# Table-lookup convolution block on one core: norm and gate matmuls in other places, a 128x128 gate, second-layer centring on GpSimd

## The chip, the cores and the metric

One NeuronCore of a Trainium2 chip runs the kernel. The metric is device time in microseconds (us) of one execution. The engines are called TensorE (PE for its matmuls, PEld for its weight loads), VectorE (DVE), ScalarE (ACT), GpSimd (POOL) and SyncE (SP, which here issues most DMAs). SBUF is the on-chip memory of 128 partitions, PSUM the eight banks that TensorE writes.

## The reference

For 16 images of 256 channels and 28x28 pixels the block is

```
x0  = group_norm(x, 32 groups)
out = relu(bn1(amm_conv3x3(x0, centroids1, wsub1)))
out = bn2(amm_conv3x3(out, centroids2, wsub2))
s   = sigmoid(relu(mean(out) @ se_w1 + se_b1) @ se_w2 + se_b2)     # 256 -> 16 -> 256
y   = x + relu(out * s + x0)
amm_conv3x3: p = 3x3 patches per channel (9 values), 16 centroids per channel
  attn = softmax(-|p - centroid|^2)            # over the 16 centroids
  lut  = centroids . wsub                      # per channel: 16 x 256
  out  = sum over channels and centroids of attn * lut
```

All is float32. The kernel does not build the lookup table: the softmax-weighted mean of a channel's centroids is a vector of nine values, and these, multiplied with `wsub`, give the same sum.

## The kernel before, in words

One image is cut into four blocks, `hh` (which 128 channels) by `t` (upper or lower half, 14 rows, N = 392 pixels). The order is `BLOCKS = ((0,0),(0,1),(1,1),(1,0))`. For a block:

- `patches` copies shifted rows of the image from DRAM (`home1`, `home2`) into one of two SBUF buffers `pts[0]`, `pts[1]`; `logits` (line 349) multiplies them with block-diagonal centroids `wd` in 32x32 tiles of TensorE into eight PSUM banks `lg`; `exps` (line 361, ACT) makes `e`.
- `num_b` (`nb`, line 410) gives the softmax sums and the ninth value, `num_a` (`na`, line 396) the other eight values in four pairs. DVE takes a reciprocal and spreads it (`rb`, lines 447 and 451). POOL multiplies (`scale_q`, line 459: `qo` and two of the `qp` pairs) and DVE the other two pairs (line 470).
- `product` (line 478, `acc`) is the convolution proper: nine 128x128 weights times the nine values. The four blocks are combined with seven products in place of eight (S1 to S4, A11, A12, A22); `mix` (lines 485 and 487, POOL) forms the differences of blocks that these need, `combine` (line 188, DVE) the sums of weights. `acc_copy`, `acc_add` (line 515) and `reg_add` put the products together (`half_sum`, `hpad`, `y`).

A PSUM bank comes from one ring of eight, which logits, numerators, products and all small matmuls share: a new one waits until the reader of the bank eight before it is done.

Every step is put on a list with `at(cluster, sub, function, ...)` and issued in order of (cluster, sub). Each engine runs its own instructions in that order. A block starts every two clusters and an image every eight, so `g = 8 * n` is the first cluster of image `n` (0 to 15 is layer 1, 16 to 31 layer 2), and sub orders the steps in a cluster: patches 0.5, logits 0.1 to 0.3, `nb` and `na` 1.0 to 1.45, spread and scale 1.7 to 1.8, product 2.0, mixes 1.75 and 2.5. So a cluster is, for TensorE: logits, then (in the even ones) `nb`, then `na`, then one product.

Beside this run, once per image or once in all:

- Group norm of the next image: `gn_stats` (line 284), `gn_mean` (a matmul of one column pair, line 290, then DVE `gn_gm`, `gn_dv` in lines 294 to 297), `gn_var` (matmul, line 303, then DVE and four small POOL operations, `rsqrt`), `gn_apply` on ACT, `to_home1`. For image 0 they stand ahead of the list, channel half by channel half.
- Squeeze and excitation in layer 2: `se_hidden` (four matmuls, line 750, and ACT) and `se_gate` (two matmuls, line 763, ACT, and DVE in lines 771 and 772).
- Centring of `wd`, so that logits need no norm of the patch: `center_sq` (square, line 251), `center_add` (matmul `sqp` with `nhalf_sb`, line 256, and addition), `center_mean` (line 261 to 263). Both halves of layer 1's weights are centred on DVE ahead of the list. Layer 2's are sorted by a ranking of the channels and centred during images 5 and 6 (`prep_wd2`, `prep_wd3`, `prep_wd4`, clusters 43 to 51).
- Loads of weights, the gate's among them, at the start on SP's and POOL's queues.

Of the kernel before, what the change touches and what calls it, by code (L numbers as in the profile page):

```python
# [8 lines left out]
F32 = mybir.dt.float32  # L9
I32 = mybir.dt.int32  # L10
U32 = mybir.dt.uint32
AF = mybir.ActivationFunctionType
# [5 lines left out]
P = 128  # L18
# [7 lines left out]
K = 16  # L26
# [41 lines left out]
def kernel(  # L68
# [80 lines left out]
    def load(ap, name, eng=None):  # L149
        t = const.tile(list(ap.shape), ap.dtype, name=name)  # L150
        (eng or nc.sync).dma_start(t, ap)
        return t
# [42 lines left out]
    load_wd(None, 1)  # L195
    load_cw(0, 1)
    vecs = load(vec, "vecs", nc.gpsimd)
    w1_sb = const.tile([P, NB, RED], F32, name="w1_sb")
    nc.gpsimd.dma_start(w1_sb, se_w1.rearrange("(b p) r -> p b r", p=P))
    w2_sb = load(se_w2, "w2_sb", nc.gpsimd)  # L200
    b1_sb = const.tile([RED, 1], F32, name="b1_sb")
    nc.gpsimd.dma_start(b1_sb, se_b1.rearrange("(p o) -> p o", o=1))

    m_lo, m_hi, zero = kst[:, 0:1], kst[:, 1:2], kst[:, 2:3]
    m_cw = kst[:, 3:7]
# [40 lines left out]

    cst = const.tile([P, 64], F32, name="cst")

    def center_sq(wf, c0, w):
        sq = rpool.tile([P, N], F32, tag="r", name="sq")  # L250
        nc.vector.tensor_mul(sq[:, :w], wf[:, c0 : c0 + w], wf[:, c0 : c0 + w])
        return sq

    def center_add(wf, c0, w, sq):
# [1 line left out]
        nc.tensor.matmul(ps[:, :w], lhsT=nhalf_sb, rhs=sq[:, :w], start=True, stop=True)  # L256
        nc.vector.tensor_add(wf[:, c0 : c0 + w], wf[:, c0 : c0 + w], ps[:, :w])

    def center_mean(wf, n):
        g = wf.rearrange("p (g k) -> p g k", k=K)  # L260
        nc.vector.tensor_reduce(cst[:, : n // K], g, axis=AX.X, op=ALU.add)
        nc.vector.tensor_scalar_mul(cst[:, : n // K], cst[:, : n // K], 1.0 / K)
        nc.vector.tensor_sub(g, g, cst[:, : n // K].unsqueeze(2).to_broadcast([P, n // K, K]))

    def center(wf, n):
        for c0 in range(0, n, 256):
# [57 lines left out]
    def to_home1(b, k, half=None):  # L324
        if k == NB - 1:
            xs.pop(b)
        p0, p1 = (0, P) if half is None else (64 * half, 64 * half + 64)
        nc.sync.dma_start(home1[b][k * P + p0 : k * P + p1], twice(xpads[k][p0:p1]))
# [41 lines left out]
    def wide_turn(u, mm):  # L370
        z = io.tile([P, 4 * N], F32, tag="pb", name="z")
        nc.vector.transpose(z, u["e", mm].rearrange("p i n -> p (i n)"))
        mx = small.tile([P, N // 4], F32, name="mx")
        zk = z.rearrange("p (g k) -> p g k", k=K)
        nc.vector.tensor_reduce(mx, zk, axis=AX.X, op=ALU.max)
        u["z", mm] = z, mx
# [296 lines left out]
            )  # L673

    def prep_wd2(part):
        pw["sq"] = center_sq(pw["st"][:, 512:1536], 384 * part, min(384, 1024 - 384 * part))

    def prep_wd3(part):
        center_add(pw["st"][:, 512:1536], 384 * part, min(384, 1024 - 384 * part), pw["sq"])

    def prep_wd4():
        st = pw.pop("st")
        center_mean(st[:, 512:1536], 1024)
        f = st[:, 512:1536].rearrange("p (g n) -> p g n", n=32)
        nc.vector.tensor_sub(f, f, kbias.unsqueeze(1).to_broadcast([P, 32, 32]))
        nc.sync.dma_start(d_wd[1], st[:, 512:1536])

    def prep_cw0():
# [55 lines left out]
    def se_hidden(b):  # L744
        ysum = ys[b, "sum"]
        ps = bank("sep")[:, :1]
        n = 0
        for k in range(NB):
            for i in range(2):
                nc.tensor.matmul(  # L750
                    ps[0:RED], lhsT=w1_sb[:, k, :], rhs=ysum[:, k, i : i + 1],
                    start=(n == 0), stop=(n == 2 * NB - 1),
                )
                n += 1
        hid = small.tile([RED, 1], F32, name="se_hid")
        nc.scalar.activation(hid, ps[0:RED], AF.Relu, bias=b1_sb, scale=1.0 / HW)
        se[b] = hid

    def se_gate(b):
# [74 lines left out]
    def at(cl, sub, f, *a, **kw):  # L834
        jobs.setdefault((cl, sub), []).append((f, a, kw))
# [54 lines left out]
    for l in range(2):  # L890
        for b in range(B):
            n = l * B + b
            g = 8 * n
            us = blocks[4 * n : 4 * n + 4]
            for c, (w, r, ks) in PRODUCTS.items():
                at(g + c, 2.0, product, (n, c), us[r], w, ks)
            for mm in (4, 2, 3, 0, 1):
                at(g + 5, 2.5, mix, us[0], mm, us[1], us[0])
                at(g + 7, 2.5 if mm < 2 else 1.75, mix, us[1], mm, us[2], us[1])
                at(*((g + 7, 2.6) if n < B - 1 else (g + 8, 1.0)), mix, us[0], mm, us[2], us[0])  # L900
                at(g + 10, 1.0, mix, us[0], mm, us[0], us[3])
            c11, c12, c21, c22 = (0, 0), (0, 1), (1, 0), (1, 1)
            at(g + 6, 0.0, acc_copy, l, b, c11, (n, 5))
            at(g + 7, 0.0, acc_copy, l, b, None, (n, 6))
            at(g + 8, 0.0, acc_add, l, b, None, (n, 7))
            at(g + 9, 0.0, acc_add, l, b, c21, (n, 8), c11)
            at(g + 10, 0.0, acc_add, l, b, c22, (n, 9), c11, pop=False)
            at(g + 10, 0.01, acc_add, l, b, c21, (n, 9))
            at(g + 10, 0.05, reg_add, l, b, c12, c22, None)
            at(g + 10, 0.06, reg_add, l, b, c22, c21, None)  # L910
            at(g + 11, 0.0, acc_add, l, b, c12, (n, 10))
            at(g + 11, 1.9, norm_out, l, b, *c12)
            at(g + 11, 1.91, norm_out, l, b, *c22)
            at(g + 12, 0.0, acc_add, l, b, c11, (n, 11))
            at(g + 12, 0.3, norm_out, l, b, *c11)
            at(g + 13, 0.0, acc_add, l, b, c21, (n, 12), op=ALU.subtract)
            at(g + 13, 0.3, norm_out, l, b, *c21)
            if l == 0:
                for o in range(2):
                    if b == 0:  # L920
                        at(g + 12 + o, 0.35, rank_score, o)
                        at(g + 12 + o, 0.6, rank_keep, o)
                        at(g + 12 + 2 * o, 0.65, h0_keep, o)
                    else:
                        for r in range(2):
                            at(g + 12 + o + (o and r), (0.5, 2.9)[r] if o == 0 else (2.4, 2.9)[r], to_home2, b, o, r)
                if b + 1 < B:
                    at(g + (-1 if b else 2), 2.6, load_x, b + 1)
                    for q in range(NB):
                        at(g + (1 + 2 * q if b else 4), 0.3, gn_stats, b + 1, q)  # L930
                    at(g + 4, 1.05 if b else 1.96, gn_mean, b + 1)
                    at(g + 4, 1.33 if b else 1.97, gn_var, b + 1)
                    for q in range(NB):
                        at(g + 5, 0.9, gn_apply, b + 1, q)
                        at(g + 5, 1.9, to_home1, b + 1, q)
            else:
                last = b == B - 1
                at(*((g + 11, 0.6) if last else (g + 13, 2.6)), load_x, b, last)
                at(g + 13, 2.1, se_hidden, b)
                at(g + (14 if last else 15), 1.05, se_gate, b)  # L940
                for q in range(NB):
                    at(g + (13 if last else 19), 0.9, finish_norm, b, q)
                    if not last:
                        at(g + 19, 0.91, finish_gate, b, q)
                        at(g + 20, 0.05, finish_sum, b, q)
                        at(g + 20, 0.9, finish_relu, b, q)
                        at(g + 21, 0.05, finish_add, b, q)
                        at(g + 21, 0.06, store, b, q)
                    else:
                        at(g + 14, 1.92, finish_fast, b, q)  # L950
                        at(g + 14, 1.92, store, b, q)
                if b == B - 1:
                    at(g + 11, 0.95, flags)
                    at(g + 12, 2.9, flag_sum)

    at(1, 0.6, load_w, 0, "A11")
    at(3, 0.6, load_w, 0, "S3")
    at(3, 0.6, load_w, 0, "A22")
    at(6, 0.6, load_w, 0, "A12")
    for c, m in ((5, "S1"), (7, "S2"), (8, "S4"), (6, "S3")):  # L960
        at(c, 1.96, combine, m)
# [21 lines left out]
    for part in range(3):  # L983
        at(43 + 2 * part, 1.9, prep_wd2, part)
        at(44 + 2 * part, 1.05, prep_wd3, part)
    at(51, 0.3, prep_wd4)
    at(52, 0.6, prep_cw0)
    at(53, 1.9, prep_cwa)
    for part in range(4):
        at((59, 60, 67, 68)[part], 2.3, prep_cwb, part)  # L990
    for n in range(5):
        at(70 + 2 * n, 0.6, sums_load, 2 * n)
        at(71 + 2 * n, 2.3, sums_put, 2 * n)
# [10 lines left out]
    at(g + 4, 0.6, load_w, 1, "A12")  # L1004
    at(g + 5, 0.6, load_w, 1, "A22")

    for k in range(NB):
        gn_stats(0, k)
        gn_mean(0, k, 1)
        gn_var(0, k, 1)  # L1010
        gn_apply(0, k)
        if k == 0:
            for i in range(2):
                to_home1(0, 0, i)
            nc.vector.memset(pts[0], 1.0)
            nc.gpsimd.memset(pts[1], 1.0)
    for hh in range(2):
        center(wts["wd", hh].rearrange("p a b c -> p (a b c)"), 512)
    at(-0.5, 0.7, to_home1, 0, 1)
    at(0, 1.95, setup_bn)  # L1020
    for t in hpads:
        at(1, 1.95, nc.gpsimd.memset, t, 0.0)

# [157 lines left out]
```

## Time and profile before

| | us |
|---|---|
| runs | 2762.52, 2751.57, 2767.31 (median 2762.52) |
| the profiled execution | 2760.28 |
| its span, first to last instruction | 2758.7 |
| busy in it: PE | 2674.9 (97%) |
| POOL | 2066.8 (75%) |
| DVE | 1732.6 (63%) |
| ACT | 1454.4 (53%) |

The profile is of one execution. A row of its timeline gives the start in us, the duration in us, engine, line, operation, output and inputs, shapes and how many instructions are merged (xN); in square brackets stands how long the engine was idle before it and what ended that. A matmul in float32 appears as two passes. Durations in groups of one kind are given as a mean in ns. PE's share of busy time says little of its speed, since matmuls overlap; what counts is when the next group can start.

### The profile page before, as it was taken

To read this page: it belongs to the slowest core of one execution; us is meant where nothing else is said; L and a number is where in the kernel's file an instruction comes from. 1 tells how busy PE (TensorE), PEld (TensorE's weight loads), DVE (VectorE), ACT (ScalarE), POOL (GpSimd) and SP (SyncE) were. 2 spreads that over 40 slices of the span, in tenths; PEclk is the share of its full clock that TensorE was granted. 3 is DMA by queue.
4 is the path that set the end of the run, shared out by engine and by line. 5 is a ranking of instruction groups with operands and counts; after the bars stand their busy time and mean duration, and the time that the engine had idled before them with its cause. 6 is when DMAs were issued, how large, how long until landed. Compare 5 with 4: busy or idle time off the path is not lost. (4 is left out here: it accounts for less than half of the span.)

```text
span 2758.7 us, 87946 instructions
## 1 busy us (share of the span) xinstructions
PE 2674.9 (97%) x37076; PEld 1297.7 (47%) x37076; DVE 1732.6 (63%) x3950; ACT 1454.4 (53%) x3277; POOL 2066.8 (75%) x1420
## 2 busy tenths in 40 slices
PE   5989999799999999999999999999999999999997
PEld 2444444344444444444444444444444444444443
DVE  5765555765555565565576766676766666766664
ACT  4444455445455445455455466656566656556653
POOL 4756787738877767766678777888877788877787
PEclk9999999999999999999999999999999999999998
DMA  9665677546677656666585455445555545555541
GB/s 202 149 135 136 165 191 184 146 107 158 154 189 189 157 128 151 158 160 150 117 183 122 105 123 122 111 104 114 114 123 123 115 104 113 116 117 123 117 105 47
DMA packets 223025, 374.51 MB, mean 136 GB/s; under 512 B 30152, under 2 KB 193336, under 8 KB 222624
## 3 DMA queue, kind: packets, MB, share of 16 engines
q1 hardware_dynamic: 215392, 334.50, 53.8%
q0 software_dynamic: 7232, 34.30, 3.6%
q8 instruction: 296, 4.85, 0.8%
q14 instruction: 105, 0.86, 0.1%
HBM read 288.91 MB, written 79.80 MB: 134 GB/s over the span
## 5 line engine op out<-in xcount | busy, mean ns | idle before, releaser
L361 ACT ACTIVATE e<-lg 128x392 f32<-128x392 f32 x1920 | 777.7, 530 | 822.7 <-PE lg L349 821.7
L487 POOL TENSOR_TENSOR qp<-qp,qp 128x784 f32<-128x784 f32 x512 | 938.2, 1862 | 41.8 <-DVE qp L470 41.8
L478 PE MATMUL acc<-qp,w_S 128*128 128x392 f32 x2048 | 709.0, 497 | 5.3 <-POOL qp L487 5.2
L459 POOL TENSOR_TENSOR qp<-qp,rb 128x784 f32<-128x784 f32 x256 | 473.0, 1869 | 253.6 <-DVE rb L451 253.6
L349 PE MATMUL lg<-pt,wd 32*32 32x392 f32 x16384 | 533.5, 503 | 28.8 <-DVE half_sum L515 17.3
L451 DVE STREAM_SHUFFLE rb<-r 128x392 f32<-128x392 f32 x1024 | 550.8, 605 | 0.0
L478 PEld LDWEIGHTS acc<-qp,w_S 128*128 128x128 f32 x2048 | 388.5, 191 | 296.7 <-POOL qp L487 10.9
L478 PE MATMUL acc<-qp,w_A 128*128 128x392 f32 x1536 | 521.3, 493 | 0.0
L396 PE MATMUL na<-e,cwa 64*32 64x392 f32 x8192 | 412.1, 498 | 10.0 <-issue 9.8
L430 DVE SCALAR_TENSOR_TENSOR r<-nb,kst,r 128x392 f32<-128x392 f32 x128 | 79.8, 624 | 517.5 <-ACT r L421 510.6
L478 PEld LDWEIGHTS acc<-qp,w_A 128*128 128x128 f32 x1536 | 292.5, 190 | 213.1
L410 PE MATMUL nb<-e,cwb 64*32 64x392 f32 x8192 | 372.2, 497 | 0.0
L349 PEld LDWEIGHTS lg<-pt,wd 32*32 32x32 f32 x16384 | 230.9, 103 | 282.8 <-issue 179.6
L436 DVE RECIPROCAL r<-r 128x392 f32<-128x392 f32 x128 | 331.9, 2593 | 0.0
L459 POOL TENSOR_TENSOR qo<-qo,rb 128x392 f32<-128x392 f32 x128 | 131.1, 1024 | 220.3 <-DVE rb L447 220.2
L470 DVE TENSOR_TENSOR qp<-na,rb 128x392 f32<-128x392 f32 x512 | 252.4, 555 | 56.1 <-PE na L396 53.1
L396 PEld LDWEIGHTS na<-e,cwa 64*32 64x32 f32 x8192 | 145.2, 106 | 234.6 <-ACT e L361 123.5
L410 PEld LDWEIGHTS nb<-e,cwb 64*32 64x32 f32 x8192 | 146.2, 107 | 209.2 <-issue 126.5
L464 ACT COPY qp<-na 128x392 f32<-128x392 f32 x512 | 211.8, 512 | 10.9 <-PE na L396 10.8
L421 ACT ACTIVATE r<-nb,kst 128x392 f32<-128x392 f32 x128 | 87.5, 684 | 102.3 <-PE nb L410 99.8
L367 ACT COPY e<-lg 128x392 f32<-128x392 f32 x128 | 52.9, 500 | 152.9 <-PE lg L349 152.9
L485 POOL TENSOR_TENSOR qo<-qo,qo 128x392 f32<-128x392 f32 x128 | 130.8, 1022 | 2.2
(143 smaller groups left out, 1778.1 us busy)
## 6 DMA issues: line engine op xcount, KB each, us to landing
pt<-home SPq DMA_DIRECT2D x768, 209.0 KB
pt<-home SPq DMA_DIRECT2D x753, 104.5 KB
home<-xpad SPq DMA_DIRECT2D x31, 899.0 KB
xt<-in_x SPq DMA_DIRECT2D x30, 784.0 KB
out_dram<-y SPq DMA_DIRECT2D x32, 392.0 KB
w_S<-d_wS SPq DMA_DIRECT2D x4, 576.0 KB
st<-in_wsub SPq DMA_DIRECT2D x4, 512.0 KB
st<-d_wa SPq DMA_DIRECT2D x16, 128.0 KB
```

What stands on the lines that cost most here:

```text
L349: nc.tensor.matmul(bk[32 * c : 32 * c + 32, :N].rearrange("p (r w) -> p r w", w=W), lhsT=wts["wd", u["hh"]][32 * i : 32 * i + 32, mm, c, : ...
L361: nc.scalar.activation(eg[:, i, :], bk[:, :N], AF.Exp, scale=2.0)
L396: nc.tensor.matmul(bs[r][32 * i : 32 * i + 32, :N], lhsT=wts["cwa", u["hh"]][64 * r : 64 * r + 64, mm, i, :], rhs=es[64 * r : 64 * r + 64, ...
L410: nc.tensor.matmul(bs[r][32 * i : 32 * i + 32, :N], lhsT=wts["cwb", u["hh"]][64 * r : 64 * r + 64, mm, i, :], rhs=es[64 * r : 64 * r + 64, ...
L436: nc.vector.reciprocal(u["r"], u["r"])
L451: nc.vector.stream_shuffle(rb[:, r, :], u["r"], mask_of(2 * mm + r))
L459: nc.gpsimd.tensor_tensor(q, q, u.pop(("rb", mm)), ALU.mult)
L464: nc.scalar.copy(u["q", 2 * mm + r], bk[:, :N])
L470: nc.vector.tensor_mul(u["q", 2 * mm + r], bk[:, :N], rb[:, r, :])
L478: nc.tensor.matmul(accs[key][:, :N], lhsT=wl[w][:, k, :], rhs=us["q", k], start=first and n == 0, stop=last and n == len(ks) - 1,)
L485: nc.gpsimd.tensor_tensor(out_u["q", 8], in0["q", 8], in1["q", 8], ALU.subtract)
L487: nc.gpsimd.tensor_tensor(pair(out_u, mm), pair(in0, mm), pair(in1, mm), ALU.subtract)
```

## The change

- The normalisation of image 0 goes half by half with the centring: norm of half 0, centring of `wd` half 0, norm of half 1; the centring of half 1 goes into cluster 0 of the list. `pts[0]` is filled with ones in two parts.
- The gate's weights are loaded in cluster 92, by SP, into 128x128 and 128x256 tiles that POOL clears before; the first of them reuses `nhalf_sb`. `se_hidden` and `se_gate` multiply with 128 rows and columns.
- `gn_mean` and `gn_var` of the next image go from `g+4` (1.05 and 1.33) to after the products of `g+3` and `g+4`; `se_gate` from `g+15`, 1.05 to after the product of `g+14`.
- In image 0 the first product goes from cluster 5 to 4, and its copy with it.
- In layer 2's centring the squares and two of the subtractions go from DVE to POOL.
- `load_w` and `load_x` of the start get other subs in their clusters; `mx` has one buffer for two.

```diff
-    w1_sb = const.tile([P, NB, RED], F32, name="w1_sb")
-    nc.gpsimd.dma_start(w1_sb, se_w1.rearrange("(b p) r -> p b r", p=P))
-    w2_sb = load(se_w2, "w2_sb", nc.gpsimd)
-    b1_sb = const.tile([RED, 1], F32, name="b1_sb")
-    nc.gpsimd.dma_start(b1_sb, se_b1.rearrange("(p o) -> p o", o=1))
+    w1_sb = [nhalf_sb, const.tile([P, P], F32, name="w1_sb")]
+    w2_sb = const.tile([P, C], F32, name="w2_sb")
+    b1_sb = const.tile([P, 1], F32, name="b1_sb")
+
+    def load_se():
+        for t in (*w1_sb, w2_sb, b1_sb):
+            nc.gpsimd.memset(t, 0.0)
+        for k in range(NB):
+            nc.sync.dma_start(w1_sb[k][:, :RED], se_w1[k * P : (k + 1) * P, :])
+        nc.sync.dma_start(w2_sb[:RED], se_w2)
+        nc.sync.dma_start(b1_sb[:RED], se_b1.rearrange("(p o) -> p o", o=1))
...
-    def center_sq(wf, c0, w):
+    def center_sq(wf, c0, w, eng=None):
-        nc.vector.tensor_mul(sq[:, :w], wf[:, c0 : c0 + w], wf[:, c0 : c0 + w])
+        (eng or nc.vector).tensor_mul(sq[:, :w], wf[:, c0 : c0 + w], wf[:, c0 : c0 + w])
...
-    def center_mean(wf, n):
+    def center_mean(wf, n, eng=None):
-        nc.vector.tensor_sub(g, g, cst[:, : n // K].unsqueeze(2).to_broadcast([P, n // K, K]))
+        (eng or nc.vector).tensor_sub(g, g, cst[:, : n // K].unsqueeze(2).to_broadcast([P, n // K, K]))
...
-        mx = small.tile([P, N // 4], F32, name="mx")
+        mx = small.tile([P, N // 4], F32, name="mx", bufs=1)
...
     def prep_wd2(part):
-        pw["sq"] = center_sq(pw["st"][:, 512:1536], 384 * part, min(384, 1024 - 384 * part))
+        pw["sq"] = center_sq(pw["st"][:, 512:1536], 384 * part, min(384, 1024 - 384 * part), nc.gpsimd)
...
-        center_mean(st[:, 512:1536], 1024)
+        center_mean(st[:, 512:1536], 1024, nc.gpsimd)
         f = st[:, 512:1536].rearrange("p (g n) -> p g n", n=32)
-        nc.vector.tensor_sub(f, f, kbias.unsqueeze(1).to_broadcast([P, 32, 32]))
+        nc.gpsimd.tensor_sub(f, f, kbias.unsqueeze(1).to_broadcast([P, 32, 32]))
...
-                    ps[0:RED], lhsT=w1_sb[:, k, :], rhs=ysum[:, k, i : i + 1],
+                    ps, lhsT=w1_sb[k], rhs=ysum[:, k, i : i + 1],
...
-        hid = small.tile([RED, 1], F32, name="se_hid")
-        nc.scalar.activation(hid, ps[0:RED], AF.Relu, bias=b1_sb, scale=1.0 / HW)
+        hid = small.tile([P, 1], F32, name="se_hid")
+        nc.scalar.activation(hid, ps, AF.Relu, bias=b1_sb, scale=1.0 / HW)
...
-                at(g + c, 2.0, product, (n, c), us[r], w, ks)
+                at(g + c - (c == 5 and n == 0), 2.0, product, (n, c), us[r], w, ks)
...
-            at(g + 6, 0.0, acc_copy, l, b, c11, (n, 5))
+            at(g + (6 if n else 5), 0.0, acc_copy, l, b, c11, (n, 5))
...
-                    at(g + (-1 if b else 2), 2.6, load_x, b + 1)
+                    at(*((g - 1, 2.6) if b else (2, 1.65)), load_x, b + 1)
                     for q in range(NB):
-                        at(g + (1 + 2 * q if b else 4), 0.3, gn_stats, b + 1, q)
-                    at(g + 4, 1.05 if b else 1.96, gn_mean, b + 1)
-                    at(g + 4, 1.33 if b else 1.97, gn_var, b + 1)
+                        at(g + (1 + q if b else 4), 0.3, gn_stats, b + 1, q)
+                    at(g + (3 if b else 4), 2.1, gn_mean, b + 1)
+                    at(g + 4, 2.1 if b else 2.2, gn_var, b + 1)
                     for q in range(NB):
-                        at(g + 5, 0.9, gn_apply, b + 1, q)
-                        at(g + 5, 1.9, to_home1, b + 1, q)
+                        at(g + 5, 0.9 if b else 0.3, gn_apply, b + 1, q)
+                        at(g + 5, 1.9 if b or q else 0.9, to_home1, b + 1, q)
...
-                at(g + (14 if last else 15), 1.05, se_gate, b)
+                at(g + 14, 1.05 if last else 2.1, se_gate, b)
...
-    at(1, 0.6, load_w, 0, "A11")
-    at(3, 0.6, load_w, 0, "S3")
-    at(3, 0.6, load_w, 0, "A22")
+    at(1, 1.65, load_w, 0, "A11")
+    at(3, 1.65, load_w, 0, "S3")
+    at(3, 1.65, load_w, 0, "A22")
...
-    at(51, 0.3, prep_wd4)
+    at(51, 1.9, prep_wd4)
...
+    at(92, 2.3, load_se)
...
-    for k in range(NB):
+    def norm0(k):
         gn_stats(0, k)
         gn_mean(0, k, 1)
         gn_var(0, k, 1)
         gn_apply(0, k)
-        if k == 0:
-            for i in range(2):
-                to_home1(0, 0, i)
-            nc.vector.memset(pts[0], 1.0)
-            nc.gpsimd.memset(pts[1], 1.0)
-    for hh in range(2):
+
+    def center_wd(hh):
         center(wts["wd", hh].rearrange("p a b c -> p (a b c)"), 512)
+
+    nc.vector.memset(pts[0][:, :4], 1.0)
+    norm0(0)
+    for i in range(2):
+        to_home1(0, 0, i)
+    nc.vector.memset(pts[0][:, 4:], 1.0)
+    nc.gpsimd.memset(pts[1], 1.0)
+    center_wd(0)
+    norm0(1)
+    at(0, 1.95, center_wd, 1)
     at(-0.5, 0.7, to_home1, 0, 1)
-    at(0, 1.95, setup_bn)
+    at(0, 1.96, setup_bn)
```

## The prediction

> **What bounds the kernel now.** I read the page first, then the busy time by stretches, then the timeline where TensorE (PE) stood still.
>
> ```profile
> PE 2674.9 (97%) x37076; PEld 1297.7 (47%) x37076; DVE 1732.6 (63%) x3950; ACT 1454.4 (53%) x3277; POOL 2066.8 (75%) x1420
> ```
>
> ```profile
> 0.00:64.00 64.00, 32.72 (x580) 14.20 (x596) 33.15 (x89) 24.91 (x55) 28.22 (x47) 0.93 0.98 207
> 535.00:562.00 27.00, 11.63 (x165) 3.83 (x164) 18.79 (x9) 4.68 (x11) 16.97 (x10) 0.62 0.35 81
> 562.00:1500.00 938.00, 934.09 (x12990) 454.97 (x12990) 566.16 (x1372) 474.69 (x1081) 686.82 (x508) 1.00 0.64 154
> 1500.00:2740.00 1240.00, 1239.38 (x17184) 606.83 (x17183) 821.61 (x1778) 718.33 (x1606) 998.87 (x601) 1.00 0.50 111
> ```
>
> The second table's columns are the stretch, its length, busy PE, weight load, DVE, ACT, POOL, then PE clock, DMA share, GB/s. From 562 us on, PE is idle for 4.5 us in 2178: there only PE's own instructions count. What waiting there is to win lies ahead of 64 us, where the DMA engines are 98% busy, and between 535 and 562 us. The timeline of that second hole, with DVE, POOL and PE in order of start (us, then duration):
>
> ```profile
> 535.52 16.73 DVE L251 TENSOR_TENSOR sq<-st 128x256 f32<-128x256 f32 x1
> ...
> 536.62 3.63 POOL L459 TENSOR_TENSOR qp<-qp,rb 128x784 f32<-128x784 f32 x2
> ...
> 544.77 7.20 POOL L487 TENSOR_TENSOR qp<-qp,qp 128x784 f32<-128x784 f32 x4
> 552.18 0.55 DVE L515 TENSOR_TENSOR half_sum<-acc,half_sum 128x392 f32<-128x392 f32 x1
> 552.78 1.53 PE L349 MATMUL lg<-pt,wd 32*32 32x392 f32 x8 [15.37 <-DVE half_sum L515]
> ```
>
> One square of 256 columns holds DVE for 16.73 us, until POOL's unbroken row of products ends at 551.97; alone the same size took 0.41 us (L251 at 14.56 us). half_sum stands behind it, and PE waits for the bank that half_sum empties.
>
> **Part 1: centring on POOL.** From lg at 535.49 to the next acc at 561.79 PE takes 26.3 us; undisturbed rows (lg 1.96, sqp 0.9, nb 2.66, na 1.48) make 7.0. The hole costs 19.3 us, the slow clock behind it included, and it goes, since no DVE square is left there. POOL's squares then come late themselves: in POOL's order each stands behind two qp products (L459). The third follows those of 536.62, which end at 540.25; at 1.02 us per 128x392 (L485) it takes 0.7 and ends at 541.0. PE wants it at 537.4, with nb and na queued behind: 3.6 us. A 3.51 us gap at 293.66 us also ran the next eight matmuls in 4.59 us instead of 2.7, so 5.5. The first square is 0.6 us late in the same way, the second is not. Net -13.2 (from -19, if POOL's backlog is gone, to -8).
>
> The Trainium skill (SBUF — State Buffer, "SBUF: two separate sides") says that a DVE instruction with two SBUF inputs and a GpSimd one that reads SBUF exclude each other for a whole instruction. The hole at 535.52 agrees; but by that rule a wait lasts one instruction, some 2 us, and part 1 would then be worth little.
>
> The two subtractions of 1024 columns also go to POOL, in image 6. Before they took DVE 1.23 us each with PE never idle. On POOL, by 1862 ns for 784 columns, they take 2.4 each (by the broadcast z row, 2.87 for 1568, 1.9), starting near 600 us. Just then DVE must do gn_dv (L296, two SBUF inputs) and behind it hpad, whose bank the next lg wants 1.5 us into its group. So gn_dv can be held 1 to 5 us: +4.5 (0 to 6.5). The d_wd store waits on SP for the second subtraction with image patches behind it; patches issued at 1100.02 in a like image serve lg at 1120.6, which covers the 4 us.
>
> **Part 2: PE's small matmuls.** Each matmul is two passes. The rows in image 16, with what follows each:
>
> ```profile
> 1533.67 0.35 PE L750 MATMUL sep<-ysum,w_sb 128*16 128x1 f32 x8
> 1533.95 2.02 PE L349 MATMUL lg<-pt,wd 32*32 32x392 f32 x64
> ...
> 1545.71 0.60 PE L763 MATMUL sep<-se_hid,w_sb 16*128 16x1 f32 x4
> 1546.24 4.22 PE L478 MATMUL acc<-qp,w_S 128*128 128x392 f32 x12
> ```
>
> se_hidden (L750) costs 0.28 us start to start, se_gate (L763) 0.53. Taking off the last pass (163 and 246 ns in the groups), the 16-column weights go at (0.35-0.163)/7 = 0.027 us a pass and the 128-column ones at (0.60-0.246)/3 = 0.118. Padding makes se_hidden eight 128-column passes: 7 x 0.091 = +0.64 (0.5 to 0.75) in each of 15 images: +9.6. In the 16th image se_hid waits for ACT's 1.96 us of xn, which covers it. Padding adds no columns to se_gate; behind a product instead of behind na its first weights can load during the last product, -0.09 to 0: -1. The group-norm pair costs 0.32 + 0.32 us plus 0.17 more of nb ahead of it and 0.02 of na; behind products 0.42 to 0.62, so -0.4 (-0.2) in 14 images: -5.5. A wait of 1.21 us at 148.03 goes with it: -1.2. Sum +1.9 (-3 to +7).
>
> The Trainium skill (TensorEngine Tiling (Array Packing), "Key Properties") says that changing the tiling mode drains TensorE, which speaks for equal shapes. In the trace acc to sep (128*16) is 6.12 us, like acc to lg, so no drain shows there beyond what lg pays anyway. The skill's TensorE: Matmul & The Clock Gate, "LDWEIGHTS", puts a load at columns / 1.2 ns, and so speaks against the padding: an estimate of 8 x 112 / 1.2 = 0.75 us an image, against 0.64 from the rows.
>
> **Part 3: the start.** Although load_w and load_x move in the schedule, SP's order of instructions stays the same up to image 6; the changes are on DVE, POOL and PE.
>
> ```profile
> 14.66 0.39 POOL L227 TENSOR_SCALAR rs_t<-gn_var 128x1 f32<-128x1 f32 x1 [2.42 <-DVE nrm L307]
> ...
> 16.30 3.50 POOL L339 DMA_DIRECT2D pt<-home  x6
> ...
> 24.67 3.21 PE L349 MATMUL lg<-pt,wd 32*32 32x392 f32 x64 [0.45 <-issue]
> ...
> 63.19 0.56 PE L303 MATMUL gnp<-gn_dv,gmat 128*128 128x2 f32 x2 [5.17 <-DVE gn_dv L297]
> ```
>
> PE loses the second centring ahead of its first lg (20.45 to 24.26). But POOL's patch loads still stand behind the second norm's rs_t, and that norm now follows a centring of 6.0 us: DVE's bn_stats start at 15.8 instead of 11.30, POOL's loads at 20.8 instead of 16.30. The third patch landed at 24.43, 6.3 us after its issue among full DMA engines; SP's six are through by 22 now, so I take 4 us (vecs landed 4.0 after issue): 26, +1.3. The late centring then sits between the first two lg groups, and the reload of pt after that: +1.7 up to cluster 4 (0 to +4.5). There the first product (6.1 us) fills the 5.17 us wait, and cluster 5 runs without it and at full clock (lg 3.37 and na 2.30 were slow): PE reaches cluster 6 at 70.6 instead of 75.32, the patches for it at 72.6. Net -2.7 (-7 to +3). Three gate loads less on POOL save 0.1: gmat was ready at 5.72, bn_aggr at 5.69.
>
> **Part 4: waits that the moves add.** In the new place gn_dv comes 0.6 us after the product ends. POOL in a steady image, then what PE and DVE did:
>
> ```profile
> 1094.40 3.65 POOL L459 TENSOR_TENSOR qp<-qp,rb 128x784 f32<-128x784 f32 x2 [6.47 <-DVE rb L451]
> ...
> 1097.97 2.02 PE L349 MATMUL lg<-pt,wd 32*32 32x392 f32 x64
> 1098.08 0.57 DVE L515 TENSOR_TENSOR hpad<-acc,hpad 128x392 f32<-128x392 f32 x1 [2.81 <-PE acc L478]
> ```
>
> POOL is done at 1098.05, gn_dv would start at 1098.6: 0.5 us clear. hpad then ends near 1099.5; PE wants its bank at 1099.7. Only four images have other POOL work there (rank_cols, prep_cwb, sums_put): +2 (0 to 6). se_gt's add meets a POOL qo product and mix of 1.0 us each in image 16 on, and POOL then waits for DVE's qp behind it, so it can lose 1.7 us at most, of which the 0.36 us that it no longer takes later and half_sum's 0.6 us of slack cover most: 0 (to +0.5 each). load_se: four small SP loads (0.5 each) wait for POOL's memsets, patches behind them; the same 20 us of lead covers it: +0.5. mx with one buffer: its reader ends 14 us before the next: 0.
>
> **Sum.** -13.2 + 4.5 + 1.9 - 2.7 + 2 + 0.5 = -7.0 against the profiled execution's 2760.28 us (span 2758.7): 2753. It lies 2 us below the median of the runs, 2762.52 (2751.57 to 2767.31). About 0.5%, 14 us, is what can be told from no change.
>
> **Rivals.** *Larger gain.* POOL's third square finds a gap, image 6 passes freely, and the first lg starts with the centring instead of with POOL's patches: -19 + 0 + 1.9 - 7 + 1 = -23, 2738. For it: the hole is the only wait over 7 us; against: POOL's rows have no gap from 532.98 to 551.97. *Slower.* gn_dv falls into POOL's pair. Place: the g + 3 cluster of 14 images. Price: up to 1.85 us for one product, and 1.9 for the clock as at 293.66, so 14 x 2.5 = +35: 2788. It decides from POOL ending 0.5 us later, or the group-norm matmul 0.5 us earlier, against each other; 14 steady images keep 0.08 to 0.13, which speaks against it, and the 0.94 us gn_dv at 602.44 shows the price. *The hole is an accident.* Eight other DVE operations got in at the end of one POOL instruction (sq of 384 columns: 1.51 us, twice). If most executions lack the hole, the change is worth -7 + 13 = +6, 2762 on the median that already lacks it.
>
> **Numbers.** Forecast 0.55 (2742 to 2764), larger gain 0.20, slower 0.12, accident 0.13. Faster by over 0.5% (below 2748.7): a quarter of the forecast's share and nearly all of the larger gain, 0.34. Slower (above 2776): 0.13. Same: 0.53. The range of 8 in 10 reaches from inside the larger gain, 2737, to 2772.
>
> **What would show it.** Right: no DVE row above 3 us; PE waiting 3 to 4 us for sqp at its third square; first lg at 26 with cluster 6 near 72.6; se_hidden at 0.9 us to lg. Wrong: gn_dv rows near 2 us in most images, or an lg that waits for hpad or half_sum in each image; or a first lg well under 24.

## The result and the profile after

The change makes the kernel slower by a quarter of a per cent: 2763.57 us median of 20 runs (2752.24 to 2776.06) against 2757.78 of 20 runs of before (2749.37 to 2767.31). The ratio is 1.0026 with an interval of 1.0013 to 1.0039, +7 us (+4 to +11); the two medians are 5.8 us apart. The forecast was 2753, 7 us faster; the range of 2737 to 2772 holds the time, the direction is wrong. The profiled execution took 2758.4 us (span 2756.9). Like the 2760.28 us of before, that is one execution out of many, so the two traces are compared place by place and not by their ends.

The page's busy times, then the busy time by stretches (stretch, length, PE, weight load, DVE, ACT, POOL, PE clock, DMA share, GB/s):

```profile
PE 2670.6 (97%) x37076; PEld 1312.1 (48%) x37076; DVE 1730.1 (63%) x3945; ACT 1454.2 (53%) x3277; POOL 2073.0 (75%) x1427
```

```profile
64.00:200.00 136.00, 109.64 (x1494) 52.13 (x1497) 99.10 (x192) 54.97 (x124) 74.42 (x54) 0.90 0.60 133
535.00:562.00 27.00, 23.74 (x371) 10.54 (x356) 13.94 (x32) 12.98 (x31) 26.15 (x18) 0.94 0.69 182
```

PE's busy time is nearly the same in total, but its idle time has moved. Between 535 and 562 us it is busy for 23.74 us, where before showed 11.63: that hole is gone, as forecast. Between 64 and 200 us it is busy for 109.64 us, and before had 125.30 there. This is the timeline of the new hole (start, duration; in brackets the idle time ahead and what ended it):

```profile
92.33 1.03 POOL L492 TENSOR_TENSOR qo<-qo,qo 128x392 f32<-128x392 f32 x1
93.21 20.26 DVE L188 TENSOR_TENSOR w_S<-w_S,w_A 128x1152 f32<-128x1152 f32 x1
93.31 3.65 POOL L494 TENSOR_TENSOR qp<-qp,qp 128x784 f32<-128x784 f32 x2
...
105.06 7.20 POOL L494 TENSOR_TENSOR qp<-qp,qp 128x784 f32<-128x784 f32 x4
113.40 0.55 DVE L522 TENSOR_TENSOR half_sum<-acc,half_sum 128x392 f32<-128x392 f32 x1
114.00 1.53 PE L356 MATMUL lg<-pt,wd 32*32 32x392 f32 x8 [18.67 <-DVE half_sum L522]
```

It is the picture of before's 535 us with another instruction in it. DVE's combine of S2 (L188) has both inputs in SBUF; a combine of this size takes 1.42 us where nothing holds it (S3's, at 86.29 us in before). Here it starts 0.14 us before a POOL instruction ends and is done only at 113.47, after POOL's unbroken row has ended at 112.26. half_sum stands behind it, and PE waits for the bank that half_sum empties. In before the same combine got in between two POOL instructions:

```profile
89.72 3.68 POOL L487 TENSOR_TENSOR qp<-qp,qp 128x784 f32<-128x784 f32 x2 [1.01 <-DVE qp L470]
92.55 2.06 DVE L188 TENSOR_TENSOR w_S<-w_S,w_A 128x1152 f32<-128x1152 f32 x1
93.35 4.80 POOL L459 TENSOR_TENSOR qp<-qp,rb 128x784 f32<-128x784 f32 x2
```

### The profile page after: what moved, and what is told of

The parts are those of the page before. It is cut to its first block, busy times and chain, and to the rows that moved or that the text cites. A ratio compares the mean times of both kernels' runs of the same rounds, so it can differ in the third digit from the quotient of the medians.

```text
span 2756.9 us, 88069 instructions
## 1 busy us (share of the span) xinstructions
PE 2670.6 (97%) x37076; PEld 1312.1 (48%) x37076; DVE 1730.1 (63%) x3945; ACT 1454.2 (53%) x3277; POOL 2073.0 (75%) x1427
```

## Experiments

Each ratio is against before on the same chip; on some chips before's median was 2757 to 2760 us, on two others 2774 to 2775. An image's time runs from its first lookup (lg) to that of the next image; images are counted from 0.

**Before, a second profiled execution** (no edit).

> The kernel before, a second profiled execution. If the hole at 535 us belongs to the kernel (theory A), DVE's first square of 384 columns takes 15 to 17 us again and image 6 lasts about 103 us; if it was an accident of one execution (theory B), the square takes under 3 us and image 6 lasts about 84. In both, image 1's combine (L188) of S2 near 92.5 us shows whether it can be caught too: over 10 us if these waits are chance, about 2 us if the order of the start decides them.

```profile
533.27 16.74 DVE L251 TENSOR_TENSOR sq<-st 128x256 f32<-128x256 f32 x1
550.55 1.53 PE L349 MATMUL lg<-pt,wd 32*32 32x392 f32 x8 [15.37 <-DVE half_sum L515]
```

It took 2758.60 us and shows the same hole to 0.01 us; image 6 lasted 101.79 us and the combine at 92 us took 2 us. (The square is the third, of 256 columns; the expectation names the first, of 384, which took 1.51 us.) All further kernels below that keep the square on DVE with two SBUF inputs show it too, eight profiles with a PE gap of 15.36 to 15.38. It belongs to the program. The rival "accident" falls.

**Centring alone.** The edit is the one in the change: `center_sq`, `center_mean` and the kbias subtraction on `nc.gpsimd`, `prep_wd4` at (51, 1.9).

> The kernel before with the second layer's centring on POOL, nothing else. Theory A (the hole at 535 us is in nearly every execution): image 6 goes from 103 to about 91 us as in the trace of the changed kernel, -12 us, 0.9956; the prediction's own sum for this part was -8.7, 0.9968. Theory B (accident): PE now waits 3 us and more for POOL's third square and 1 us for hpad behind gn_dv, without a gain: +4 to +7 us, 1.0015 to 1.0025.

Measured 2744.04 us, 0.9956 (0.9939 to 0.9973): -12 us, theory A. Image 6 takes 90.43 us, and PE waits 3.27 us for POOL's third square.

**Padding alone.** Padded tiles, `load_se`, `mx` with one buffer; `se_gate` stays.

> The kernel before with the gate weights padded to 128x128 and loaded at cluster 92, se_gate in its old place. By the prediction's step: +0.64 us in each of 15 images and +0.5, +10.1 us, 1.0037; by the changed kernel's trace (se_hidden 0.88 us to lg after 0.28): +0.60 x 15 = +9, 1.0033. Rival: equal shapes spare TensorE a drain in each of the two places, then the loss is under +4 us, 1.0015. In the start nothing should differ but three POOL loads less (-0.1 us).

Measured 1.0021 (1.0008 to 1.0034), +5.8 us; the interval holds the rival's 1.0015 and the 1.0033 of the second estimate alike, so the trace has to decide. A steady image of layer 2 went from 82.29 to 82.79 us: se_hidden costs 0.60 more, but the product ahead of it 0.09 less (6.03 instead of 6.12) and se_gate 0.06 less. So something is spared where shapes are equal, as the rival said, 0.15 of the 0.60 us, not most of it.

**The group-norm pair alone, twice.**

```
-  at(g + (1 + 2 * q if b else 4), 0.3, gn_stats, b + 1, q)
-  at(g + 4, 1.05 if b else 1.96, gn_mean, b + 1)
-  at(g + 4, 1.33 if b else 1.97, gn_var, b + 1)
+  at(g + (1 + q if b else 4), 0.3, gn_stats, b + 1, q)
+  at(*((g + 3, 2.1) if b else (g + 4, 1.96)), gn_mean, b + 1)
+  at(g + 4, 2.1 if b else 1.97, gn_var, b + 1)
```

> The kernel before with the group-norm pair of images 2 to 15 moved behind the lookups' products, nothing else. By the prediction: -0.4 us in 14 images and -1.2 for the wait at 148 us, +2 for gn_dv meeting POOL: -4.7 us, 0.9983; by the changed kernel's trace (steady period 82.31 to 81.83): -0.48 x 14 - 1.2 = -8 us, 0.9971. Rival: gn_dv falls into POOL's pair in most images, +35 us, 1.013.

> The kernel with the group-norm move alone, a second profiled execution. The first one took 2755.26 us, the lowest of its twelve (median 2761.75). If the usual execution has a wait that the first lacked, this one shows it: an image of layer 1 that lasts 5 us or more longer than in the first (image 1's combine over 10 us, or gn_dv over 3 us). If image times agree within 1 us, the difference is the clock.

Measured 1.0017 (1.0005 to 1.003): +4.7 us where -4.7 was forecast. In the first profile a steady image of layer 1 does go from 82.31 to 81.83 us, but image 6 lasts 105.81 us (102.88 and 101.79 in the two profiles of before; part of it is a wait of PE for hpad behind gn_dv, 1.25 us) and image 8 84.38 (82.43 and 82.41). That execution was the fastest of the twelve, 2755.26 us, so its trace does not hold the loss of the median. The second execution ran on a chip where before takes 2774.23 us, and took 2769.63. Its profile shows neither 5 us in one image nor only the clock, but one slow lookup in each of images 10 to 14. This is the one in image 11:

```profile
1044.34 3.28 PE L349 MATMUL lg<-pt,wd 32*32 32x392 f32 x64
1047.55 2.86 PE L410 MATMUL nb<-e,cwb 64*32 64x392 f32 x64
```

From lg to nb is 3.21 us; 1.96 is usual. On the same chip the kernel with the start alone, group norm in its old place, shows 2.52 at the like place, so the move adds 0.7 there and takes 0.5 away. This goes by the chip: at that place in image 11 the eight kernels profiled on the two slower chips take 2.5 us without the move and 3.0 to 3.2 with it, and all twelve profiles from elsewhere 1.96, with the move or without. The profile names no wait in it; why is open.

**The reordered start alone**, and with the S2 combine, then S2 and S4, on POOL. The start is `norm0`/`center_wd`, the first product at cluster 4, the first loads, and image 1's norm at 2.1 and 2.2. The other edits:

```
-  nc.vector.tensor_tensor(wl[n], wl[a], wl[b], op)
+  (nc.gpsimd if n == "S2" else nc.vector).tensor_tensor(wl[n], wl[a], wl[b], op)         # start_s2
+  (nc.gpsimd if n in ("S2", "S4") else nc.vector).tensor_tensor(wl[n], wl[a], wl[b], op)  # start_pool
```

> The kernel before with the reordered start alone: norm of half 1 behind the centring of half 0, second centring behind the first lookup, first product one cluster earlier, image 1's norm later. The square hole at 535 us stays. By the prediction's step: -2.7 us, 0.999. Theory A (the reorder brings image 1's combine of S2 into POOL's unbroken row in every execution, as at 93.21 us in the changed kernel): image 1 lasts 111 to 114 us instead of 101, the time is +10 to +14 us, 1.0035 to 1.005. Theory B (that wait was an accident of one execution): the combine takes 2 us, and the time is +1 to +4 from the first lookup alone, 1.001.

> The same reordered start, with the combine of S2 on POOL instead of DVE, so that no DVE operation with two SBUF inputs stands there. Theory A: image 1's long wait goes, -10 us or more against the kernel with the start alone, and what is left of the start is -1 to +4 us against before, 0.9995 to 1.0015; POOL's 2.7 us for the combine stay off the path. Theory B: no difference beyond 3 us between the two.

> The reordered start with the combines of S2 and of S4 both on POOL; with S2 alone there, the next combine (S4) was shut out for 12 us instead and PE still waited 6.4 us. If the holes at the combines are what the start costs, no DVE operation is over 5 us in image 1, PE's wait of 19 us at 114 us (start alone) and of 6.4 us at 120 us (S2 on POOL) are gone, and the time is within 2 us of before or below it, 0.9985 to 1.0005, against 1.0066 and 1.0015. Rival: the late first lookup (28.3 instead of 24.7 us) is the loss, then it stays at 1.001 to 1.002.

Measured 1.0066 (1.005 to 1.0082), 1.0015 (1.0004 to 1.0027) and 1.0018 (1.0009 to 1.0027). The start alone costs 18 us, with the combine shut out for 20.22 us. Off DVE that goes, 14 us, but the next candidate is caught: with S2 on POOL the combine of S4, with both on POOL a DVE operation of another kind, and PE waits 6.41 and 4.35 us for hpad behind them. The two, each from its kernel:

```profile
107.42 12.18 DVE L188 TENSOR_TENSOR w_S<-w_A,w_S 128x1152 f32<-128x1152 f32 x1
```

```profile
118.83 6.87 DVE L562 TENSOR_SCALAR c<-c 128x144 f32<-128x144 f32 x1
```

So the third run's expectation of no row over 5 us failed, and these runs alone could not price the late first lookup.

**The two halves of the start.** One kernel takes `norm0`, `center_wd` and `setup_bn` from the change, the other the early product, the loads and image 1's norm.

> Of the reordered start only the order of DVE's norm and centring: norm of half 1 behind the centring of half 0, second centring behind the first lookup; first product, loads and image 1's norm as before. Theory C (the late norm is the loss): POOL's rs_t is held 2.1 us at 7.9 us again, the first lookup starts at 28 to 29.5 us instead of 24.7, the wait of 5.2 us at 63 us stays, and image 1 begins 4 us late: +4 to +5 us, 1.0015 to 1.002, and more (1.006) if its combine of S2 is shut out too. Theory D (the late norm costs nothing that the later waits do not cover): within 1 us.

> Of the reordered start only the first product one cluster earlier and image 1's norm later; DVE's norm and centring as before. The product fills the wait of 5.2 us at 63 us. Theory C: the first lookup stays at 24.7 us and image 1 begins 4 to 5 us earlier, -4 to -5 us, 0.9984, unless a DVE combine of image 1 falls into POOL's row, which costs 11 to 18 us and would show as a DVE row over 5 us there (1.003 to 1.005). Theory D: no difference.

Measured 1.0015 (1.0004 to 1.0025) and 1.0047 (1.0034 to 1.006). Theory C, with its exception. The combine in the first kernel, then in the second:

```profile
99.33 2.07 DVE L188 TENSOR_TENSOR w_S<-w_S,w_A 128x1152 f32<-128x1152 f32 x1
```

```profile
92.65 20.21 DVE L188 TENSOR_TENSOR w_S<-w_S,w_A 128x1152 f32<-128x1152 f32 x1
...
113.39 1.53 PE L349 MATMUL lg<-pt,wd 32*32 32x392 f32 x8 [19.23 <-DVE half_sum L515]
```

The late norm costs 4 us: first lookup at 28.03, the 5.2 us wait still there at 70.30. The early product (with the loads and image 1's norm) does fill that wait: 0.74 us of it is left, and cluster 6 starts at 72.81 us instead of 75.32. But in that cluster PE then waits for POOL (0.90 and 0.88 us), and image 1 begins at 92.23 us, where before began it at 91.23: theory C's gain is not there. And it costs 13 us, because POOL is at another point of its row when the combine arrives, 0.11 us ahead of the end of a POOL instruction.

**The same out of the changed kernel.** `product`, `acc_copy`, `load_x`, `load_w` and image 1's norm back in their old places, the rest of the change kept.

> The changed kernel with its first product, first loads and image 1's norm put back where they were before; everything else of the change stays. The early product alone cost 0.47% by shutting out the combine of S2 in image 1; if it does the same inside the changed kernel, the combine here takes 2 to 3 us, image 1 lasts 98 to 101 us instead of 112.7, and the time is 1.0026 - 0.0047 = 0.998 of before. If the parts do not add (the late norm alone already shifts the combine into POOL's row there), it stays at 1.002 to 1.003.

Measured 2751.46 us, 0.997 (0.9958 to 0.9982).

```profile
100.42 2.07 DVE L188 TENSOR_TENSOR w_S<-w_S,w_A 128x1152 f32<-128x1152 f32 x1
101.24 4.78 POOL L466 TENSOR_TENSOR qp<-qp,rb 128x784 f32<-128x784 f32 x2
```

The combine slips in between two POOL products (POOL's pair then takes 4.78 instead of 3.61 us), image 1 lasts 98.13 us instead of 112.74, and the change is worth having. This one piece (the early product with the loads and the norm of image 1 that go with it) is 0.56% of the time, twice the whole loss.

**What shuts DVE out.** The third square stays on DVE at its place, but one of its inputs comes from PSUM:

```
+  ps = bank("sqc")
+  nc.scalar.copy(ps[:, :256], wf)
-  nc.vector.tensor_mul(sq[:, :256], wf, wf)
+  nc.vector.tensor_mul(sq[:, :256], wf, ps[:, :256])
```

> The kernel before, with one thing changed: for the third square (256 columns) ACT copies the slice to a PSUM bank first, and DVE multiplies the SBUF slice by that bank, so that the DVE operation reads one SBUF input instead of two. It stays on DVE, at the same place beside POOL's unbroken row. If it is the second SBUF input that shuts DVE out while POOL streams, the square takes under 1 us, the 15 us gap of PE goes and the time falls by 14 to 18 us (0.994 to 0.995), more than with the centring on POOL, which pays 3.3 us of waiting for POOL's square. Rival: POOL's row shuts out any DVE operation on SBUF at that place; then the operation takes 16 us again and the time is that of before.

Measured 0.9934 (0.9921 to 0.9947), -18 us, image 6 in 84.63 us.

```profile
534.58 3.69 POOL L487 TENSOR_TENSOR qp<-qp,qp 128x784 f32<-128x784 f32 x2
537.11 0.42 DVE L683 TENSOR_TENSOR sq<-st,sqc 128x256 f32<-128x256 f32 x1
```

In the middle of a POOL instruction, 1.16 us ahead of its end (1.14 in before), the square takes 0.42 us, not 16.7. The second SBUF input is what waits.

**Combinations.** `se_gate` one place earlier with the weights unpadded; the group-norm pair beside the centring; both; the pair beside the PSUM square.

> Centring on POOL, and se_gate one place earlier with its 16-column weights as they were; old start, old group norm. From the traces the earlier se_gate is worth 0.22 us in each image of layer 2 (steady image 82.79 us with padding alone, 82.57 in the changed kernel): -12.0 - 3.3 = -15 us, 0.9944. By the prediction's -1 for se_gate: -13, 0.9952.

> Centring on POOL and the group-norm pair behind the products together, old start, old gate. If the two add up as measured alone (-12.3 and +4.4): -8 us, 0.997. If the loss of the group-norm move comes from image 6, where DVE's backlog behind the square holds gn_dv and hpad (PE waited 1.25 us at 597 us, image 6 lasted 105.8 instead of 102 us), it goes with the hole, and the steady images' -0.48 us each shows: -12.3 - 5 to -7 = -17 to -19, 0.9935.

> The same with the group-norm pair behind the products as well: all of the change but the reordered start and the padding. If the group-norm move is worth nothing on this chip (with the centring it brought 0.9953 against 0.9956): 0.994 as the kernel without it. If its -0.48 us an image counts: -21 us, 0.992. If it costs what it cost alone (+0.17%): 0.996.

> The third square with its PSUM input and the group-norm pair behind the products. If the group-norm move's loss alone (+0.17%) came from image 6, where gn_dv and hpad stand behind the shut-out square: 0.991, -0.48 us an image. If it comes from the steady images, where one lookup then took 3.2 instead of 1.96 us: 0.994 to 0.995, no better than the square alone, and PE's groups show that lookup in each image.

Measured 0.9957 (0.9944 to 0.9971), 0.9953 (0.9935 to 0.9971), 0.9953 (0.9939 to 0.9966) and 0.993 (0.9914 to 0.9947). Beside the centring (0.9956) or the PSUM square (0.9934), se_gate and the group-norm move bring nothing that can be told from zero. (The second and third ran on the two slower chips, where the moved pair has its slow lookups.) In the last kernel the steady images have their gain (81.84 us), and images 7 to 9 take 85.82, 86.12 and 85.07 us, among them a PE wait of 3.58 us for the patch DMA at 785 us.

**The early product without its trap.**

```
-  for c, m in ((5, "S1"), (7, "S2"), (8, "S4"), (6, "S3")):
+  for c, m in ((5, "S1"), (6, "S3"), (6, "S2"), (8, "S4")):
```

> The third square with its PSUM input (0.9934 alone) and the first product one cluster earlier. If both count: 0.9917. If the combine is shut out with the earlier product: 0.997.

> The third square with its PSUM input and the early product (0.9967 together), with the combine of S2 one cluster earlier, right behind that of S3. If the combine finds POOL between its products there, the hole of 20 us in image 1 goes and the early product's gain of some 4 us shows: 0.992. If it is shut out at the new place too, a DVE row over 5 us stands in image 1 and the time is 0.995 to 0.998.

Measured 0.9967 (0.9955 to 0.9979) with the combine at its old place in the list, shut out for 20.20 us, and 0.9925 (0.9906 to 0.9944) with it one cluster earlier, where it takes 2.3 us. This last one, 2742.51 us beside 2759.66 of before, has the lowest ratio of all; it can't be told from the PSUM square alone. The time met the 0.992 of the expectation, but its reason, a gain of 4 us by the early product, is not in the trace: image 2 begins at 195.61 us, after 192.54 in before. Now the combine of S4 is held, for 4.90 us, and PE waits 2.29 us for hpad behind it.

## Why the prediction was wrong, point by point

| step | forecast, us | measured alone, us |
|---|---|---|
| centring on POOL, image 6 included | -13.2 + 4.5 | -12.1 |
| padding, load_se | +9.6 + 0.5 | +5.8 |
| se_gate earlier | -1 | 0 |
| group-norm pair, with its waits | -5.5 - 1.2 + 2 | +4.7 |
| start | -2.7 | +18.3 |
| sum | -7.0 | +16.7 |

The measured column is each ratio's excess times before's median on its chip, with some 4 us of uncertainty either way; se_gate's is the difference of two kernels. The whole change measures +7, not +17: the parts do not add. One possible reason is that the group-norm pair costs nothing beside the centring (-13.0 against -12.1, on different chips, each with some 5 us either way); the rest of the difference is within the intervals. That the range holds the time is in part luck: the start came out 21 us worse than forecast and the group-norm pair 9, centring and padding 3 and 4 us better, and the parts together cost less than their sum.

*Start: the step that failed.* "-2.7 (-7 to +3)" priced the late norm and the early product by what PE waits for up to cluster 6, and stopped there; alone the start measures +18. The prediction knew that a DVE instruction with two SBUF inputs can be lost behind POOL's row, at 535 us. It did not ask it of the combines at 72 to 107 us, which the early product moves against POOL, though three of their four rows in before (2.06 to 2.81 us for 1.42) already showed them waiting. The hole was not removed, it came back at another instruction: +13 us for the early product alone, 15 us inside the change.

The late norm was mis-sized too: +1.3 for the first lookup, at 26; it came at 28.94 (28.03 in the kernel with the late norm alone). POOL's patch loads came at 20.29, no later than the 20.8 of the forecast; but the third of them, for which 4 us were allowed, landed at 28.70, 6.6 us after its issue (6.3 in before). The forecast had SP's loads through by 22 us; between 22 and 29 us the queue on which they run still moved 1.31 MB. These rows show why SP was late, which was not in the sum:

```profile
7.83 2.11 POOL L234 TENSOR_SCALAR rs_t<-gn_var 128x1 f32<-128x1 f32 x1 [2.79 <-DVE nrm L314]
8.11 1.46 DVE L1028 MEMSET pt<- 128x1680 f32 x1 [0.30 <-issue]
9.48 0.36 DVE L258 TENSOR_TENSOR sq<-wd 128x256 f32<-128x256 f32 x1
...
28.94 3.35 PE L356 MATMUL lg<-pt,wd 32*32 32x392 f32 x64 [10.57 <-DMA home<-xpad]
```

rs_t, of one column, took 0.24 us in before. Here POOL gets it done only when DVE's memset and square are over, the home writes leave SP at 12.30 instead of 10.51 and SP's patch loads at 16.51 instead of 14.72. The product at cluster 4 filled the 5.17 us wait (0.74 is left at 69.44), but PE then waits 2.30 us for patches, and cluster 6 started at 75.70, not 72.6: nothing gained there either.

*Centring: right.* The hole's 19.3 us went; PE waits 3.26 us for the third square, forecast 3.6, and the slow clock behind it (0.67 granted from 553.4 to 558.3 us) makes nb 3.81 instead of 2.66:

```profile
553.48 1.22 PE L263 MATMUL sqp<-sq,nhalf_sb 128*128 128x256 f32 x2 [3.26 <-POOL sq L258]
...
554.63 3.81 PE L417 MATMUL nb<-e,cwb 64*32 64x392 f32 x64
```

Mis-sized was the +4.5 for the subtractions: gn_dv is held for 1.75 us at 597.85, and PE waits 0.94. The rule of the Trainium skill (SBUF — State Buffer, "SBUF: two separate sides"), that a loser waits for the other's instruction, fits neither hole: DVE waits for a whole row of instructions. Its half that speaks of two SBUF inputs is what the PSUM square confirms.

*Padding: right in kind.* se_hidden in the changed kernel:

```profile
1529.49 0.50 PE L757 MATMUL sep<-ysum,nhalf_sb 128*128 128x1 f32 x4
1529.85 0.58 PE L757 MATMUL sep<-ysum,w_sb 128*128 128x1 f32 x4
1530.36 2.02 PE L356 MATMUL lg<-pt,wd 32*32 32x392 f32 x64
```

Eight passes in 0.87 us, 0.28 before: the 0.64 forecast was 0.6. In the trace layer 2 pays 0.28 an image in all (82.57 for 82.29), 0.22 less than with padding alone, since a product ahead of an equal shape and the gate behind one are each 0.1 us quicker. The earlier place alone, with unpadded weights, brings 0.02 (82.27). So the rival of equal shapes was worth half of the 0.6, which the sum left out; whether that is a drain no run shows.

*Group norm: the wrong sign, cause not settled.* The -0.4 an image was right in the traces of the faster chips (-0.48 in the changed kernel), and the feared meeting of gn_dv and POOL does not happen in the steady images. What takes it back stays open. Seen are longer images 6 to 9 (some 5 us together in the first profile) and, on the two slower chips, a lookup that is slow with no wait named.

*Rivals.* "Slower" had the right side and the wrong mechanism and place: not gn_dv in 14 images but one combine. "Larger gain" would have needed the start. "The hole is an accident" came nearest with its +6, but by luck: the hole stands in all ten profiles whose square reads SBUF twice. Two sums among the rivals are off without touching the forecast: -23 from 2760.28 makes 2737, and +6 on 2762.52 makes 2768.

## What to carry to other kernels

An instruction that waits behind another engine's unbroken row is a property of the moment at which it arrives: before moving anything, list every DVE instruction with two SBUF inputs that lies beside POOL's rows, and ask of each, not only of the one that is stuck now, where the move puts it. Giving one of its inputs a home in PSUM removed the wait where moving the work to POOL only exchanged it for a smaller one (image 6 in 84.63 us against 90.43; the ratios, 0.9934 and 0.9956 on different chips, overlap in their intervals). A gain summed from PE's waits up to one point is not a gain until the stretch behind that point has been followed too.

## What the runs showed of the hardware

- A DVE instruction that was shut out did not get in at the next end of a POOL instruction. In two places it got in only when POOL paused: 16.7 us past nine ends for a square of 0.4, 20.2 us past eleven for a combine of 1.4. Both repeat to 0.06 us from kernel to kernel. A pause is not always needed: the S4 combine of 12.18 us got in past six ends while POOL's next instruction was already issued and waited in its turn (2.12 us instead of 1.0).
- What decides whether it gets in at the first end is open. The S2 combine got in where it came 0.84 to 0.87 us before a POOL instruction ended, and was shut out in all four kernels where it came 0.10 to 0.14 us before. But S4's combine came 0.91 and 0.99 us before and the square 1.14, and all three were shut out, while other combines came at 1.1 and got in.
- DVE's tensor_scalar with one tensor input can be shut out as well (6.87 us; 0.98 in before), and a POOL instruction of one column took 2.11 us instead of 0.24 while DVE's memset and square ran. The Trainium skill (SBUF — State Buffer, "Who interferes with whom") counts tensor_scalar among the operations that can take the shared ports, which agrees. The shuffles, reciprocals and batch statistics show no such wait in the trace of before: reciprocals of 392 columns took 2.59 to 2.60 us beside POOL and without it, shuffles 0.58 to 0.65.
- PE stands still for 1.3 to 3.3 us ahead of one na group between 1125 and 1171 us in 14 of the 20 traces, with nothing named but issue (2.09 and 2.51 in the two of before). What it waits for was not found.
